# Deformable sampling in single rounds: two PSUM banks cut in quarters, and the steps behind a round set two rounds apart

## The chip, the core and the metric

The kernel runs on one core of one Trainium2 chip. The metric is the device time of one launch in microseconds (us); three runs of the kernel before gave 8797.73, 8817.04 and 8818.68 us, median 8817.04. A core has five engines that each work through their own queue in order: PE (TensorE, matrix products into PSUM), DVE (VectorE), ACT (ScalarE), POOL (GpSimd, here the issuer of gathers) and SP (SyncE, the issuer of plain DMAs). They wait for one another by semaphores, which the Tile framework sets from what each instruction reads and writes.

## What is computed

Four layers on a batch of 4 images of 256 channels and 64 x 64 positions: a block with deformable convolution, linear attention, a 3 x 3 convolution with binarised weights, and a non-local attention block. The change is in the first layer. There each position takes, in each of 4 channel groups, 9 points of a projected image at places that were computed from the data, each by bilinear interpolation, with a softmax weight, and sums them:

```python
x = x + _L0_conv_ref(_gn(x), ...)

# in _L0_conv_ref, of one image in one of G = 4 groups, P = 9 points a position
def tap(xi, yi, w):
    valid = (xi >= 0) & (xi < Wi) & (yi >= 0) & (yi < Hi)
    idx = jnp.clip(yi, 0, Hi - 1) * Wi + jnp.clip(xi, 0, Wi - 1)
    v = jnp.take_along_axis(flat, idx.reshape(B, 1, -1), axis=2)
    v = v.reshape(B, Cc, *xi.shape[1:])
    return v * (w * valid.astype(img.dtype))[:, None]
return tap(x0, y0, (1 - wx) * (1 - wy)) + tap(x0 + 1, y0, wx * (1 - wy)) + tap(x0, y0 + 1, (1 - wx) * wy) + tap(x0 + 1, y0 + 1, wx * wy)

samp = _grid_sample(img, sg)
dout = (samp * mr).sum(-1).reshape(n, G * GC, H * W).transpose(0, 2, 1).reshape(n, H, W, C)
dout = jnp.einsum('nhwc,oc->nhwo', dout, outproj_w) + outproj_b
x2 = _bn(inp + dout, bn2_g, bn2_b, bn2_m, bn2_v, 3)
```

## The kernel before, in words

**Stages.** `run` samples the four images one after another. Beside each sampling, other work is woven in by shares: with image 0 the convolutions and offsets of the other images, with image n the feed-forward and the linear layer of image n - 1, and from image 2 on also the convolution and the attention block of image n - 2. What is left of the last images follows alone. The function `beside` calls the generator `sample` for one round, then lets the other generators go on until they have spent their share, then asks for the next round. Within this part the order of PE, DVE, ACT and POOL is the order in which the program issues instructions (`manual_schedule`); no engine overtakes within its queue.

**A round.** `sample` (L556) takes the 4096 positions of an image in blocks of 224 (`BP`), the last one of 64. A block has 16 rounds of 14 positions (`RP`), the last block 5, with 8 positions in the fifth; so 293 rounds an image and 1172 in all. 14 positions x 9 points are 126 rows. `gathered` (L596) issues four indirect DMAs on POOL (L600), one for each group, which fetch four neighbours of 64 channels for each of the rows into a tile `g` (seven buffers). Then PE multiplies (L607) a sparse weight matrix `wm` (made by DVE at L591 once in four rounds) with `g`: eight products, two accumulating into each of four strips of 32 partitions. The result, 128 x 128 numbers, is a round's sums in `acc`.

**The steps behind a round.** They work on units of two rounds (`UR = 2`). `acc` and `dp` are one PSUM bank each (512 numbers a partition), a single tile cut in two halves that units take in turn (`halves`, L565). For a unit whose last round is number i:

- `moved` (L610): ACT copies the half of `acc` to `at` in SBUF, 128 x 256 (L612). Issued at the start of round i + 1.
- `turned` (L614): PE transposes both rounds of `at` into a half of `dp` (L617). Issued at the start of round i + 2.
- `spread` (L619): ACT copies them to their places in `dT`, the block's transposed sums, in two copies for the two halves of the partitions, 64 x 112 each (L632). Issued at round i + 3, for the first unit of a block one round later. The first one of a block also allots the block's tiles and lets SP load the block of `y`.
- At the end of a block, `project` (L636, PE with the output weights, L640), `add` (DVE, L644) and `finish` (ACT with the batch norm, L649, and the store to `x2_d` on SP, L652), for the two halves of the channels m = 0, 1: project at i + 4 + m, add and finish one and two rounds after it.

`later` (L563) holds, for each round, the list of steps that are due; they are issued at the start of that round ahead of its gathers and matmuls (L658), in the order in which they were put there.

Around the change stand the instructions of the other streams: in the feed-forward PE at L742 and L752, ACT at L744 and DVE at L727; in the linear layer the 25 taps of a depthwise convolution on DVE (L178), transposes and their copies (L862, L863 on PE, L865 on ACT) and products (L869); ACT copies at L823; in layer 2 the products at L1048; in layer 3 the products of the attention (L1147, L1167) and, before them, a PSUM tile whose columns 0 to 127 are written by L1119 and read by ACT at L1122, and whose columns 128 to 255 are written by L1121 and read by DVE at L1123.

Of the kernel before, what the change touches and what calls it, by code (L numbers as in the profile page):

```python
# [9 lines left out]
F32 = mybir.dt.float32  # L10
# [7 lines left out]
P = 128  # L18
N, C, H, W = 4, 256, 64, 64
HW = H * W  # L20
KT = C // P
NB = HW // 512
NT = HW // P
G, PT = 4, 9
# [2 lines left out]
NCH = NT // CT  # L27


RP, WR, UR, BR = 14, 4, 2, 16  # L30
RS, BP = RP * PT, RP * BR
BLOCKS = [(p0, min(BP, HW - p0)) for p0 in range(0, HW, BP)]
OB = 16
# [38 lines left out]
class Net:  # L72
# [483 lines left out]
    def sample(self, n, ssum):  # L556

        nc, sp = self.nc, self.sp
        table = self.tab[n].rearrange("g y x s c -> (g y x) (s c)")
        blocks, images, at, dp, dT, po, later = {}, {}, {}, {}, {}, {}, {}  # L563

        def halves(name):  # L565

            t = self.ps1.tile([P, 2, 256], F32, name=name, tag=name)
            return cycle([t[:, 0], t[:, 1]])

        accs, dps = halves("acc"), halves("dp")  # L570

        def load(b):
            p0, np_ = BLOCKS[b]
            whole, part = np_ // RP, np_ % RP

            nr = whole + (part > 0)
            sl = sp.tile([P, BR, G * 5], F32, name="sl")
            rows = self.s_d[n][p0 * PT:p0 * PT + nr * RS, :].rearrange("(r p) f -> p r f", p=RS)
            more = self.s_d[n][p0 * PT + RS:p0 * PT + (nr + 1) * RS, :].rearrange("(r p) f -> p r f", p=RS)
            nc.sync.dma_start(sl[0:RS, 0:nr], rows)  # L580
            nc.sync.dma_start(sl[RS:P, 0:nr], more[0:P - RS])
            rounds = [(r, RP) for r in range(whole)] + [(whole, part)] * (part > 0)
            blocks[b] = sl, rounds

        def weigh(b, r):

            sl, rounds = blocks[b]
            nu = min(WR, len(rounds) - r)
            wm = self.gp.tile([P, WR, 4 * G, OB], F32, name="wm")
            sh = [P, nu, 4 * G, OB]  # L590
            nc.vector.tensor_tensor(  # L591
                wm[:, 0:nu], self.con("own").unsqueeze(1).unsqueeze(1).to_broadcast(sh),
                sl[:, r:r + nu, G:].unsqueeze(3).to_broadcast(sh), ALU.mult)
            return wm

        def gathered(sl, wm, acc, r):  # L596
            r4, acc = r % WR, acc[:, r % UR * P:(r % UR + 1) * P]
            g = self.gp.tile([P, G, 256], F32, name="g", bufs=7)
            for i in range(G):
                nc.gpsimd.indirect_dma_start(  # L600
                    out=g[:, i, :], out_offset=None, in_=table,
                    in_offset=bass.IndirectOffsetOnAxis(ap=sl.bitcast(I32)[:, r, i:i + 1], axis=0))


            for x in range(2):
                for i in range(G):
                    nc.tensor.matmul(acc[32 * i:32 * i + 32, :], wm[:, r4, 4 * i + 2 * x:4 * i + 2 * x + 2, :],  # L607
                                     g[:, i, x * P:(x + 1) * P], start=x == 0, stop=x == 1)

        def moved(acc, nu, u):  # L610
            at[u] = sp.tile([P, UR, P], F32, name="at")
            nc.scalar.copy(at[u].rearrange("p v c -> p (v c)")[:, 0:nu * P], acc[:, 0:nu * P])  # L612

        def turned(nu, u):  # L614
            dp[u] = next(dps).rearrange("p (v g s o) -> p v g s o", v=UR, g=G, s=2)
            for v in range(nu):
                nc.tensor.transpose(dp[u][:, v].rearrange("p g s o -> p (g s o)"), at[u][:, v], self.ident)  # L617

        def spread(unit, b, u):  # L619

            if b not in dT:
                p0, np_ = BLOCKS[b]
                dT[b] = sp.tile([P, G, BP], F32, name="dT", bufs=1)
                images[b] = sp.tile([P, KT, BP], F32, name="yb")
                nc.sync.dma_start(images[b][:, :, 0:np_], self.y_d[n][:, :, p0:p0 + np_])
            full = sum(1 for _, m in unit if m == RP)
            for v0, v1, m in ((0, full, RP), (full, len(unit), unit[-1][1])):
                for s in range(2):
                    if v0 < v1:
                        hs = slice(64 * s, 64 * s + 64)  # L630
                        q0 = RP * (unit[0][0] + v0)
                        nc.scalar.copy(  # L632
                            dT[b][hs, :, q0:q0 + m * (v1 - v0)].rearrange("p g (v o) -> p g v o", o=m),
                            dp[u][hs, v0:v1, :, s, 0:m].rearrange("p v g o -> p g v o"))

        def project(b, m):  # L636
            np_ = BLOCKS[b][1]
            po[m] = self.ps("po")
            for k in range(G):
                nc.tensor.matmul(po[m][:, 0:np_], self.ow[:, k, m * P:(m + 1) * P], dT[b][:, k, 0:np_], start=k == 0, stop=k == G - 1)  # L640

        def add(b, m):
            ym = images[b][:, m, 0:BLOCKS[b][1]]
            nc.vector.tensor_tensor(ym, po[m][:, 0:BLOCKS[b][1]], ym, ALU.add)  # L644

        def finish(b, m):
            p0, np_ = BLOCKS[b]
            ym = images[b][:, m, 0:np_]
            nc.scalar.activation(ym, ym, AF.Identity, bias=self.sh[:, 4 + m:5 + m],  # L649
                                 scale=self.inv[:, 4 + m:5 + m], accum_out=ssum[:, m, b:b + 1])  # L650
            if m == KT - 1:
                nc.sync.dma_start(self.x2_d[n][:, :, p0:p0 + np_], images[b][:, :, 0:np_])  # L652

        load(0)
        order = [(b, r) for b, (_, np_) in enumerate(BLOCKS) for r in range(-(-np_ // RP))]
        wm = weigh(0, 0)
        for i, (b, r) in enumerate(order):
            for f in later.pop(i, ()):  # L658
                f()
            sl, rounds = blocks[b]  # L660
            if r % UR == 0:
                acc = next(accs)
            gathered(sl, wm, acc, r)
            if r == 0 and b + 1 < len(BLOCKS):
                load(b + 1)
            ends = r + 1 == len(rounds)
            if r % WR == 0:
                if r + WR < len(rounds):
                    nxt = weigh(b, r + WR)
                elif b + 1 < len(BLOCKS):  # L670
                    nxt = weigh(b + 1, 0)
            if r % UR == UR - 1 or ends:
                unit = rounds[r - r % UR:r + 1]
                todo = [partial(moved, acc, len(unit), i), partial(turned, len(unit), i), partial(spread, unit, b, i)]

                todo = [(i + 1 + j + (j == 2 and r < UR), f) for j, f in enumerate(todo)]
                if ends:
                    todo += [(i + 4 + m + j, partial(f, b, m)) for m in range(KT) for j, f in enumerate((project, add, finish))]
                for j, f in todo:
                    later.setdefault(j, []).append(f)  # L680
            if r % WR == WR - 1 or ends:
                wm = nxt
            yield 1
        for i in sorted(later):
            for f in later[i]:
                f()
# [656 lines left out]
```

## The profile before

One profiled execution spans 8805.8 us from its first to its last instruction; the median of the runs is 8817.04 us, so about 11 us lie around the span.

| row of the profile | count | busy us | mean ns | idle before it, us |
|---|---|---|---|---|
| L600 POOL gather | 4688 | 4618.5 | 985 | 2687.8 |
| L607 PE products into acc | 18752 records | 1034.8 | 333 | 1907.8 |
| L612 ACT acc to at, 128 x 256 | 584 | 217.3 | 372 | 985.5 |
| L612 ACT acc to at, 128 x 128 | 4 | 1.1 | 265 | 0.8 |
| L617 PE transposes | 1172 | 284.1 | 330 | 106.6 |
| L632 ACT dp to dT, 64 x 112 | 1168 | 284.4 | 244 | 1041.5 |
| L632 ACT dp to dT, 64 x 32 | 8 | 1.4 | 179 | 2.2 |
| L178 DVE depthwise taps | 2280 | 2933.5 | 1287 | 61.9 |

How to read it: busy is the sum of the bars of a row, and idle the time in which its engine stood still just before them. A row's idle time is ended by another instruction (the releaser), which the profile infers from semaphore events: "PE acc L607 <- ACT at L612: 1273.7, 281, 27.6" means that PE stood still before L607 until the copy at L612 was done, 1273.7 us in all, 281 times, once for 27.6 us. "remote" is a release for which no instruction close in time is seen, "issue" a gap that nothing shown explains. Gaps under 150 ns are not counted. PEld are PE's weight loads, which overlap its products; the two are waited for together, so a list that sums both counts a wait twice. By stretches, with a gather count in brackets in the POOL column (four are a round):

| from to, us | PE busy | DVE busy | ACT busy | POOL busy | granted PE clock |
|---|---|---|---|---|---|
| 250 to 1950 | 826.64 | 757.57 | 244.13 | 1112.59 (1116) | 0.66 |
| 2450 to 3600 | 609.83 | 809.98 | 213.54 | 764.77 (781) | 0.69 |
| 4200 to 5480 | 926.65 | 965.52 | 333.96 | 798.70 (821) | 0.85 |

The gathers stand between 134.1 and 7306.6 us.

### The profile page before, as it was taken

The page shows a single profiled execution, that of the slowest core. Times are in us where ns is not written, and L with a number is a line of the kernel's source. Part 1 is how long each engine was busy: PE and PEld are TensorE (multiplying, and loading weights), DVE is VectorE, ACT ScalarE, POOL GpSimd, SP SyncE. Part 2 cuts the span into 40 slices and gives each one's busy share as a digit, 9 for nine tenths or more (in the row PEclk, how much of TensorE's full clock was granted, in tenths as well). Part 3 has the DMA queues.
Part 4 walks back from the last instruction along what each step waited for, and adds up shares of the span by engine and source line. Part 5 has one row for each costly group of instructions (what it writes and reads, how often), then busy time and mean ns, then how long its engine had stood idle before and what let it go on. Part 6 is the DMA issues. An engine that isn't in the chain of part 4 may idle for free. (4 is left out here: it accounts for less than half of the span.)

```text
span 8805.8 us, 95736 instructions
## 1 busy us (share of the span) xinstructions
PE 5993.9 (68%) x36532; PEld 3575.6 (41%) x36532; DVE 5173.3 (59%) x6409; ACT 2183.8 (25%) x4899; POOL 5152.4 (59%) x4950
## 2 busy tenths in 40 slices
PE   4454554448744446688876677888766778986899
PEld 2222222224323322244544443345544433664477
DVE  5444443443466667424777776227777772599834
ACT  1111111112211112122223222222222222465524
POOL 2666666566666666666666656666666661376410
PEclk7676766669866667799988888898878888998999
DMA  6454454444433334444443344444434343220131
GB/s 172 127 155 124 141 154 118 125 145 145 153 105 105 110 105 129 127 130 138 134 135 110 112 121 136 142 134 132 136 115 117 114 118 99 69 74 29 48 98 53
DMA packets 759050, 1042.27 MB, mean 118 GB/s; under 512 B 362432, under 2 KB 472128, under 8 KB 757056
## 3 DMA queue, kind: packets, MB, share of 16 engines
q0 software_dynamic: 225024, 614.77, 24.3%
q1 hardware_dynamic: 533568, 421.39, 16.4%
q8 instruction: 289, 4.73, 0.2%
q14 instruction: 169, 1.38, 0.0%
HBM read 867.08 MB, written 168.69 MB: 118 GB/s over the span
## 5 line engine op out<-in xcount | busy, mean ns | idle before, releaser
L600 POOL DMA_INDIRECT g<-tab,sl x4688 | 4618.5, 985 | 2687.8 <-issue 1224.2
L178 DVE SCALAR_TENSOR_TENSOR agg<-pad,vec,agg 128x1024 f32<-128x1024 f32 x2280 | 2933.5, 1287 | 61.9
L607 PE MATMUL acc<-g,wm 128*32 128x128 f32 x18752 | 1034.8, 333 | 1907.8 <-ACT at L612 1273.7
L607 PEld LDWEIGHTS acc<-g,wm 128*32 128x32 f32 x18752 | 566.8, 128 | 2411.7 <-ACT at L612 1446.1
L1048 PE MATMUL ps<-xd,w 128*128 128x256 f32 x3072 | 752.7, 396 | 51.3 <-issue 37.8
L591 DVE TENSOR_TENSOR wm<-con,sl 128x1024 f32<-128x1024 f32 (+1 forms) x296 | 357.7, 1209 | 711.9 <-remote 533.5
L1048 PEld LDWEIGHTS ps<-xd,w 128*128 128x128 f32 x3072 | 595.1, 199 | 175.0 <-issue 86.0
L632 ACT COPY dT<-dp 64x112 f32<-64x112 f32 x1176 | 285.9, 243 | 1043.7 <-remote 544.3
L742 PE MATMUL ps<-x2f,f 128*128 128x512 f32 x1024 | 499.2, 636 | 19.1 <-issue 7.7
L817 PE MATMUL ps<-xr,qw 128*128 128x512 f32 x768 | 472.0, 746 | 22.1 <-issue 11.1
L727 DVE SCALAR_TENSOR_TENSOR hm<-ps,vec,lk 128x512 f32<-128x512 f32 x256 | 190.8, 750 | 492.9 <-ACT lk L744 405.5
L752 PE MATMUL ps<-hm,f 128*128 128x512 f32 x1024 | 467.1, 605 | 0.9 <-DVE hm L727 0.9
L612 ACT COPY at<-acc 128x256 f32<-128x256 f32 (+1 forms) x588 | 218.3, 371 | 986.3 <-remote 753.2
L999 POOL TENSOR_TENSOR xd<-xp 128x640 f32<-128x640 f32 x64 | 79.4, 1268 | 492.6 <-ACT xp L1011 298.3
L640 PE MATMUL po<-dT,ow 128*128 128x224 f32 (+1 forms) x1216 | 326.1, 419 | 45.4 <-issue 19.3
L617 PE MATMUL dp<-ident,at 128*128 128x128 f32 x1172 | 284.1, 330 | 106.6 <-ACT dT L632 61.0
L865 ACT COPY kt<-pt 128x512 f32<-128x512 f32 x256 | 149.4, 584 | 829.3 <-remote 403.8
L744 ACT ACTIVATE lk<-ps,low 128x512 f32<-128x512 f32 x256 | 174.0, 687 | 666.0 <-PE ps L742 512.1
L1147 PE MATMUL s<-ph,th 128*128 128x512 f32 x512 | 290.2, 672 | 62.5 <-ACT kt L865 15.9
L640 PEld LDWEIGHTS po<-dT,ow 128*128 128x128 f32 x1216 | 265.5, 233 | 113.8 <-issue 68.9
L1167 PEld LDWEIGHTS ps<-gt,pT 128*128 128x128 f32 x2048 | 276.0, 213 | 70.8 <-issue 46.1
L194 POOL TENSOR_TENSOR ak<-ak,m 128x1024 f32<-128x1024 f32 x96 | 228.1, 2376 | 130.6 <-ACT m L193 126.7
(243 smaller groups left out, 8022.0 us busy)
## 6 DMA issues: line engine op xcount, KB each, us to landing
g<-tab,sl POOLq DMA_INDIRECT x4688
x<-x SPq DMA_DIRECT2D x128, 512.0 KB
xr<-x SPq DMA_DIRECT2D x96, 512.0 KB
tab<-xo SPq DMA_DIRECT2D x192, 128.0 KB
x<-in_x SPq DMA_DIRECT2D x32, 512.0 KB
y<-yc SPq DMA_DIRECT2D x32, 512.0 KB
x2f<-x SPq DMA_DIRECT2D x32, 512.0 KB
xyf<-x SPq DMA_DIRECT2D x32, 512.0 KB
```

The lines of the kernel that those rows point to most:

```text
L178: nc.vector.scalar_tensor_tensor(to, s, wt, acc, ALU.mult, ALU.add)
L591: nc.vector.tensor_tensor(wm[:, 0:nu], self.con("own").unsqueeze(1).unsqueeze(1).to_broadcast(sh), sl[:, r:r + nu, G:].unsqueeze(3).to_bro ...
L600: nc.gpsimd.indirect_dma_start(out=g[:, i, :], out_offset=None, in_=table, in_offset=bass.IndirectOffsetOnAxis(ap=sl.bitcast(I32)[:, r, i: ...
L607: nc.tensor.matmul(acc[32 * i:32 * i + 32, :], wm[:, r4, 4 * i + 2 * x:4 * i + 2 * x + 2, :], g[:, i, x * P:(x + 1) * P], start=x == 0, st ...
L617: nc.tensor.transpose(dp[u][:, v].rearrange("p g s o -> p (g s o)"), at[u][:, v], self.ident)
L632: nc.scalar.copy(dT[b][hs, :, q0:q0 + m * (v1 - v0)].rearrange("p g (v o) -> p g v o", o=m), dp[u][hs, v0:v1, :, s, 0:m].rearrange("p v g ...
L640: nc.tensor.matmul(po[m][:, 0:np_], self.ow[:, k, m * P:(m + 1) * P], dT[b][:, k, 0:np_], start=k == 0, stop=k == G - 1)
L742: nc.tensor.matmul(ps, f1[:, k, m * P:(m + 1) * P], x2[:, k], start=k == 0, stop=k == KT - 1)
L752: nc.tensor.matmul(ps, f2[:, k, m * P:(m + 1) * P], hm[:, k], start=k == 0, stop=k == 4 * KT - 1)
L817: nc.tensor.matmul(ps, qw[:, k, m * P:(m + 1) * P], x[:, k], start=k == 0, stop=k == KT - 1)
L1048: nc.tensor.matmul(ps[:, e], w[:, k, t, 2 * half + e, m * P:(m + 1) * P], v[:, 2 * half + e, k, t:t + 8], start=i % 6 == 0, stop=i % 6 == 5)
L1147: nc.tensor.matmul(s[i], tv[:, 4 * b + j], ph[:, i * 512:(i + 1) * 512], start=True, stop=True)
```

## The change

Units of two rounds are gone: every round has its own copy, transpose and spreading. `acc` and `dp` stay a bank each, a single tile, now cut in four quarters of one round. The copy of round i is issued at the start of round i + 2, its transpose at i + 4, its spreading at i + 6 (rounds 0 and 1 of a block at 8 rounds after them, and at 7), and `project`, `add`, `finish` at i + 7 + m and one and two rounds after, for i the last round of a block. `at` has three buffers of 128 x 128 for two of 128 x 256.

```diff
-RP, WR, UR, BR = 14, 4, 2, 16
+RP, WR, BR = 14, 4, 16
+MOVED, TURNED, SPREAD, PROJECTED = 2, 4, 6, 7
...
-        def halves(name):
+        def quarters(name):
 
-            t = self.ps1.tile([P, 2, 256], F32, name=name, tag=name)
-            return cycle([t[:, 0], t[:, 1]])
+            t = self.ps1.tile([P, 4, P], F32, name=name, tag=name)
+            return cycle([t[:, i] for i in range(4)])
 
-        accs, dps = halves("acc"), halves("dp")
+        accs, dps = quarters("acc"), quarters("dp")
...
-            r4, acc = r % WR, acc[:, r % UR * P:(r % UR + 1) * P]
+            r4 = r % WR
...
-        def moved(acc, nu, u):
-            at[u] = sp.tile([P, UR, P], F32, name="at")
-            nc.scalar.copy(at[u].rearrange("p v c -> p (v c)")[:, 0:nu * P], acc[:, 0:nu * P])
-
-        def turned(nu, u):
-            dp[u] = next(dps).rearrange("p (v g s o) -> p v g s o", v=UR, g=G, s=2)
-            for v in range(nu):
-                nc.tensor.transpose(dp[u][:, v].rearrange("p g s o -> p (g s o)"), at[u][:, v], self.ident)
-
-        def spread(unit, b, u):
+        def moved(acc, u):
+            at[u] = sp.tile([P, P], F32, name="at", bufs=3)
+            nc.scalar.copy(at[u], acc)
+
+        def turned(u):
+            t = next(dps)
+            nc.tensor.transpose(t, at.pop(u), self.ident)
+            dp[u] = t.rearrange("p (g s o) -> p g s o", g=G, s=2)
+
+        def spread(b, r, m, u):
...
-            full = sum(1 for _, m in unit if m == RP)
-            for v0, v1, m in ((0, full, RP), (full, len(unit), unit[-1][1])):
-                for s in range(2):
-                    if v0 < v1:
-                        hs = slice(64 * s, 64 * s + 64)
-                        q0 = RP * (unit[0][0] + v0)
-                        nc.scalar.copy(
-                            dT[b][hs, :, q0:q0 + m * (v1 - v0)].rearrange("p g (v o) -> p g v o", o=m),
-                            dp[u][hs, v0:v1, :, s, 0:m].rearrange("p v g o -> p g v o"))
+            for s in range(2):
+                hs = slice(64 * s, 64 * s + 64)
+                nc.scalar.copy(dT[b][hs, :, RP * r:RP * r + m], dp[u][hs, :, s, 0:m])
...
-            if r % UR == 0:
-                acc = next(accs)
+            acc = next(accs)
             gathered(sl, wm, acc, r)
...
-            if r % UR == UR - 1 or ends:
-                unit = rounds[r - r % UR:r + 1]
-                todo = [partial(moved, acc, len(unit), i), partial(turned, len(unit), i), partial(spread, unit, b, i)]
-
-                todo = [(i + 1 + j + (j == 2 and r < UR), f) for j, f in enumerate(todo)]
-                if ends:
-                    todo += [(i + 4 + m + j, partial(f, b, m)) for m in range(KT) for j, f in enumerate((project, add, finish))]
-                for j, f in todo:
-                    later.setdefault(j, []).append(f)
+            todo = [(MOVED, partial(moved, acc, i)), (TURNED, partial(turned, i)), (SPREAD + max(0, KT - r), partial(spread, b, *rounds[r], i))]
+            if ends:
+                todo += [(PROJECTED + m + j, partial(f, b, m)) for m in range(KT) for j, f in enumerate((project, add, finish))]
+            for j, f in todo:
+                later.setdefault(i + j, []).append(f)
```

## The prediction

> **What bounds the kernel now.** I read the page first (busy times, slices, groups), then the totals of waits, then the timeline of a few rounds, then single lines of code.
>
> The page and the totals of waits:
>
> ```profile
> span 8805.8 us, 95736 instructions
> PE 5993.9 (68%) x36532; PEld 3575.6 (41%) x36532; DVE 5173.3 (59%) x6409; ACT 2183.8 (25%) x4899; POOL 5152.4 (59%) x4950
> L600 POOL DMA_INDIRECT g<-tab,sl x4688 | 4618.5, 985 | 2687.8 <-issue 1224.2
> ...
> PE acc L607 <- ACT at L612: 1273.7, 281, 27.6
> POOL g L600 <- remote: 624.7, 307, 6.0
> POOL g L600 <- PE acc L607: 494.3, 201, 23.2
> ```
>
> No engine is full. Sampling runs from about 134 to 7340 us, 1172 rounds (4688 gathers of four a round), and is 82% of the span. A round's gathers cost POOL at least 4 x (985 + 305 ns) = 5.16 us (305 ns is 1224.2 / 4007, the gap it always has), so 6048 us for all of them; the real pace is (7306.6 - 134.1) / 1172 = 6.12 us. The missing 0.96 us a round is POOL waiting for a free g buffer, which PE frees: the lines "remote" and "PE acc" sum to 1119 us. So PE paces the sampling and POOL follows, seven buffers ahead. And PE's largest wait is the one for the copy at L612. In the timeline:
>
> ```profile
> 2721.80 0.58 ACT L865 COPY kt<-pt 128x512 f32<-128x512 f32 x1 [5.32 <-remote]
> 2721.92 0.94 POOL L600 DMA_INDIRECT g<-tab,sl  x1 [1.83 <-remote]
> 2722.28 0.50 ACT L632 COPY dT<-dp 64x112 f32<-64x112 f32 x2
> 2722.81 0.37 ACT L612 COPY at<-acc 128x256 f32<-128x256 f32 x1
> ...
> 2723.23 1.08 PE L607 MATMUL acc<-g,wm 128*32 128x128 f32 x16 [5.99 <-ACT at L612]
> ...
> 2725.26 0.63 PE L617 MATMUL dp<-ident,at 128*128 128x128 f32 x2
> ...
> 2725.83 1.08 PE L607 MATMUL acc<-g,wm 128*32 128x128 f32 x16
> ```
>
> The matmuls at 2723.23 open a unit. They write the half of the bank that the copy at 2722.81 does not read; their own half was copied a whole unit before. Still they start 50 ns after this copy ends. The second round of the unit (2725.83) waits for nobody. That is the rule and no accident: of the line L607 the trace says
>
> ```profile
>   ACT at L612: 2719.8, 588
> ```
>
> 588 is every unit (PE and weight loads counted together). So the wait is by bank, not by half. The same holds in the other direction, for a read after a write elsewhere in the bank. In layer 3, L1122 reads columns 0 to 127 (written by L1119), L1123 reads 128 to 255 (written by L1121):
>
> ```profile
> L1122 ACT ACTIVATE ph<-ps,fw_add x32: 366/367/378, 4546.1 to 8635.6; 128x128 f32<-128x128 f32 x32
> ...
>   PE ps L1121: 23.8, 17
> ...
>   DVE gt L1123: 43.1, 11
> ```
>
> The read of the first quarter waits for the matmul into the second, and the read of the second waits for the read of the first.
>
> **What the Trainium skill says.** "PSUM — Partial Sum Buffer", PSUM bank collisions: two engines may not touch one bank (in the same partitions) at once, even at different addresses, so waits are to be set by bank; this trace agrees (588 of 588, above). "Perfetto Trace Analysis", Tensor Engine Instruction: the end of a matmul in a profile is computed, and its semaphore comes later, unseen; the trace agrees, for the many waits that end with "remote" end well after the last matmul shown. So a chain PE to ACT to PE costs more than the bars say. "TensorE: Matmul & The Clock Gate", Part 1: a PE idle for some 3.4 us falls to half its clock; here the granted clock is 0.66 from 250 to 1950 us, where PE is busy half the time, and 0.85 from 4200 to 5480. More waiting lengthens what PE does next.
>
> **The change part by part.** Both banks stay one tile each, now in four quarters. In round i the kernel issues, in this order: spread(i-6), two ACT copies out of dp; turned(i-4), a transpose into dp; moved(i-2), an ACT copy out of acc; then the eight matmuls of round i into acc.
>
> *The wait on acc.* By bank, moved(i-2) waits for the matmuls of round i-1, the last writers of its bank, and the matmuls of round i wait for moved(i-2). The distance of two rounds is thus undone; each copy stands between two neighbouring rounds. Before, it stood there once in two rounds: 588 times. Now 1172 times, so 584 are new.
>
> *The wait on dp.* turned(i-4) waits for spread(i-6), spread for turned(i-5). Before, at the odd round, both were long past (L617 waited 61.0 us in all for L632). Now PE meets ACT here too, but at the point where it would wait for moved right after, so this adds order, not a second full wait.
>
> *ACT's work.* Copies: 1172 x 265 ns (the four 128x128 ones there are) = 310.6, for 218.3 now: +92 us. Spreads: 2344 of 64x56 for 1176 of 64x112. The rows have 179 ns for 64x32 and 244 for 64x112, so about 198 ns: 465 for 286, +179 us. ACT at 25% has room, but these stand in its queue just ahead of what PE waits for.
>
> *PE's and POOL's work.* 1172 transposes, 18752 matmul records and 4688 gathers, as before: nothing. Gathers and the wm products (L591) are not moved.
>
> *The sum.* When ACT comes on time, a meeting costs PE the stretch from the first spread to the first matmul: 2722.28 to 2723.23 = 0.95 us a unit now. After: 2 x 0.198 + 0.265 + 0.08 of gaps = 0.74 a round, 1.48 for two rounds. That is +0.53 us x 588 = +312 us. Behind each image the deeper pipeline drains without rounds between, six stages for two, about a meeting each: 4 x 0.74 x 4 images = +12 us. POOL's waits show that lateness of PE reaches the gathers, so I count it whole: +325 us.
>
> Bounds: below, 0, if ring and ACT's idle time swallow it. Above, each new meeting costs what a present one does, when ACT is late with its other queue (kt, lk, v copies stand ahead of it): 1273.7 / 588 = 2.17 us, x 584 = +1265 us. I don't take that, because much of it is ACT's backlog of two rounds, which would be met half at a time. What waits behind the stopped PE: the transposes and products of the feed-forward, linear and convolution streams, and through L742 to L744 and L727 DVE. Behind the stopped ACT: the same streams' copies.
>
> *Moves.* Projection, add and finish come three rounds later; the loads of y (SP) and the stores of x2 with them, both a block (16 rounds) from use. The new spread waits for the last project of the block before, as now one round back. Both at nothing; if SP were late, add would show it.
>
> The profiled span is 8805.8, the median of the runs 8817.0, 11 us more. 8805.8 + 325 + 11 = 9142, say 9150 us.
>
> **The rivals.**
>
> A, forecast, one meeting a round at about its bare price: 9150 (own range 8950 to 9500). Chance 0.50.
>
> B, full price. ACT is late as often as now, at every round: 8817 + 1265 = 10080. For: half of PE's openings wait, with 4.5 us each (1273.7 / 281). Against: ACT's backlog is halved. With values between A and B, 0.16.
>
> C, swallowed. POOL's 5.16 us a round stays the floor and PE's new stops fall where it stood idle anyway: in 250 to 1950 PE is busy 49% and yet the pace is 6.09 us, in 4200 to 5480 72% at 6.24, so the pace hardly follows PE's load. 8817 to 8930. Chance 0.21, of which 0.06 within 0.3%, 0.02 slightly faster.
>
> D, faster: the waits are by quarter after all. Then moved(i-2) finds its matmuls done a round ago, and ACT never stops for the newest ones (753.2 + 141.0 us before L612 now), nor PE for the newest copy (1273.7). Gain at most POOL's 1119 us of waiting; a third, since PE's other waits remain: 8817 - 370 = 8450. It decides if fewer than half of the rounds wait for their newest neighbour. Against: 588 of 588 and L1122. Chance 0.13.
>
> **How the numbers follow.** Faster 0.13 + 0.02 = 0.15; same 0.06; slower 0.50 + 0.16 + 0.13 = 0.79. About 0.3% (26 us) is what a measurement here can tell from no change. The range leaves out D (0.13) and the upper part of B (0.07): 8800 to 9700 us.
>
> **What would show it.** Right: L607 waits for the copy some 1172 times, with more than 1273.7 us; the new copies take about 265 and 198 ns; POOL's "remote" and "PE acc" grow by about what the span grows. A wrong: the count stays near 588, or it doubles and POOL's waits don't grow (C), or the mean wait stays 2.2 us (B). Wrong altogether: PE's waits for ACT shrink (D), or the copies are far from the prices.

## The result and the profile after

The changed kernel takes 8942.99 us (median of 4 runs, 8916.39 to 8947.37), the kernel before 8817.86 (8797.73 to 8839.72) measured beside it. The medians differ by 125 us. The ratio is put at 1.0126 with a 95% interval of 1.0102 to 1.0151, that is 90 to 133 us. The forecast had the sign, and the wait for the newest copy, but counted 325 us.

The page of the changed kernel; a row has count, busy us and mean ns, and after the bar the idle time of the engine ahead of it with what ended most of it:

```profile
span 8940.6 us, 98293 instructions
PE 6060.7 (68%) x36532; PEld 3589.3 (40%) x36532; DVE 5177.0 (58%) x6409; ACT 2415.7 (27%) x6651; POOL 5164.5 (58%) x4950
...
L601 POOL DMA_INDIRECT g<-tab,sl x4688 | 4631.3, 988 | 2808.2 <-issue 1210.8
...
L608 PE MATMUL acc<-g,wm 128*32 128x128 f32 x18752 | 986.8, 340 | 1041.5 <-ACT at L613 709.3
L617 PE MATMUL dp<-ident,at 128*128 128x128 f32 x1172 | 421.1, 359 | 1238.5 <-ACT dT L629 902.5
...
L613 ACT COPY at<-acc 128x128 f32<-128x128 f32 x1172 | 311.6, 266 | 1717.6 <-remote 1262.5
...
L629 ACT COPY dT<-dp 64x56 f32<-64x56 f32 x2344 | 466.2, 199 | 630.2 <-remote 261.5
```

ACT works 231.9 us more and still only 27% of the span. The two copies cost 266 and 199 ns, where 265 and 198 were estimated. PE's stop has moved: most of it now stands ahead of the transpose (1238.5 us, 106.6 before) and less ahead of the products (1041.5, 1907.8 before). Together 2280.0 us, 265.6 more than the 2014.4 of before.

From the totals of waits of the changed kernel (us in all, times, longest):

```profile
PE dp L617 <- ACT dT L629: 902.5, 340, 17.2
PE acc L608 <- ACT at L613: 709.3, 187, 28.6
POOL g L601 <- PE acc L608: 623.2, 237, 30.4
POOL g L601 <- remote: 587.4, 300, 5.8
```

POOL's two waits for a free buffer sum to 1210.6 us, 91.6 more than before. One round in the timeline shows the meeting (start, duration, engine, line; in brackets the idle time and what ended it):

```profile
4704.32 0.40 ACT L629 COPY dT<-dp 64x56 f32<-64x56 f32 x2
...
4704.74 0.27 ACT L613 COPY at<-acc 128x128 f32<-128x128 f32 x1
...
4704.77 0.47 PE L617 MATMUL dp<-ident,at 128*128 128x128 f32 x1 [1.54 <-ACT dT L629]
...
4705.18 1.08 PE L608 MATMUL acc<-g,wm 128*32 128x128 f32 x16
...
4706.56 0.95 POOL L601 DMA_INDIRECT g<-tab,sl  x1 [7.79 <-PE acc L608]
```

PE stands until both spreads are done, transposes while ACT copies, and starts the products after the copy: 0.86 us from the first spread to the first product, 0.74 in the estimate. The whole trace shows the same order: in all 1164 rounds that have such a copy ahead of them (the first two of each image have none) the products start after it has ended, in 610 of them within 0.1 us. Before, all 587 openings of a unit did so, 428 within 0.1 us. So the mechanism is there, in every round.

Where the time went is seen by stretches. POOL's counts in brackets, almost all gathers (four a round), tell how far each kernel came in the same stretch; the stretches are the first three images of the kernel before. Kernel before, then changed kernel:

```profile
134.00:1949.00 1815.00, 853.55 (x6730) 491.38 (x6734) 797.73 (x1062) 250.10 (x695) 1189.60 (x1195) 0.65 0.48 136
1949.00:3703.00 1754.00, 1048.70 (x6865) 549.29 (x6865) 1048.42 (x1046) 343.85 (x877) 1159.32 (x1173) 0.74 0.42 123
3703.00:5522.00 1819.00, 1366.94 (x8670) 819.14 (x8669) 1147.13 (x1373) 453.97 (x1108) 1144.58 (x1173) 0.87 0.44 128
```

```profile
134.00:1949.00 1815.00, 840.83 (x6692) 491.24 (x6692) 794.41 (x1051) 300.85 (x1120) 1181.37 (x1187) 0.64 0.48 136
1949.00:3703.00 1754.00, 1061.27 (x6763) 548.91 (x6764) 1049.23 (x1046) 397.01 (x1296) 1141.39 (x1156) 0.73 0.41 121
3703.00:5522.00 1819.00, 1351.97 (x8489) 806.92 (x8488) 1138.63 (x1362) 504.63 (x1514) 1120.28 (x1141) 0.86 0.43 126
```

(columns: us, then busy time and count of PE, weight loads, DVE, ACT and POOL, then PE's granted clock, DMA share and GB/s.) In the stretch of image 0 the changed kernel falls 8 gathers behind, in image 1 17, in image 2 32. The loss grows with what runs beside the sampling. Read from the start of the last round of each image, the four samplings became longer by 16, 20, 47 and 47 us, 131 in all. The rest of the span, after the last round, went from 1476.0 to 1479.9 us.

### The profile page after: what moved, and what is told of

Its sections match the earlier page's. It is cut to its first block, busy times and chain, and to the rows that moved or that the text cites. A ratio compares the mean times of both kernels' runs of the same rounds, so it can differ in the third digit from the quotient of the medians.

```text
span 8940.6 us, 98293 instructions
## 1 busy us (share of the span) xinstructions
PE 6060.7 (68%) x36532; PEld 3589.3 (40%) x36532; DVE 5177.0 (58%) x6409; ACT 2415.7 (27%) x6651; POOL 5164.5 (58%) x4950
## 5 line engine op out<-in xcount | busy, mean ns | idle before, releaser
L608 PE MATMUL acc<-g,wm 128*32 128x128 f32 x18752 | 986.8, 340 | 1041.5 <-ACT at L613 709.3
L617 PE MATMUL dp<-ident,at 128*128 128x128 f32 x1172 | 421.1, 359 | 1238.5 <-ACT dT L629 902.5
L608 PEld LDWEIGHTS acc<-g,wm 128*32 128x32 f32 x18752 | 554.8, 130 | 1377.8 <-ACT at L613 841.1
L617 PEld LDWEIGHTS dp<-ident,at 128*128 128x128 f32 x1172 | 188.0, 160 | 1678.9 <-ACT dT L629 1151.9
L613 ACT COPY at<-acc 128x128 f32<-128x128 f32 x1172 | 311.6, 266 | 1717.6 <-remote 1262.5
L629 ACT COPY dT<-dp 64x56 f32<-64x56 f32 x2344 | 466.2, 199 | 630.2 <-remote 261.5
```

The costliest lines, as they stand in the source:

```text
L617: nc.tensor.transpose(t, at.pop(u), self.ident)
L629: nc.scalar.copy(dT[b][hs, :, RP * r:RP * r + m], dp[u][hs, :, s, 0:m])
```

## The experiments

All ratios are against the kernel before, run in the same group of runs on the same chip; intervals in brackets are 95%. This matters here: on the chips of e1 to e8 and e13 to e16 the kernel before took 8764 to 8826 us, on that of e9 to e12, e17 and e18 7739 us. So runs of different groups are compared by ratio, or not at all.

### What a meeting costs: its length, its number, its distance

**e1.** ACT's finer instructions in the kernel before.

```diff
-            nc.scalar.copy(at[u].rearrange("p v c -> p (v c)")[:, 0:nu * P], acc[:, 0:nu * P])
+            for v in range(nu):
+                nc.scalar.copy(at[u][:, v], acc[:, v * P:(v + 1) * P])
...
-            for v0, v1, m in ((0, full, RP), (full, len(unit), unit[-1][1])):
+            for v0, v1, m in [(v, v + 1, unit[v][1]) for v in range(len(unit))]:
```

> The kernel before, with ACT's instructions cut as fine as in the changed kernel (the copy of a unit in two of 128x128, the spreads in four of 64x56), in the same places, so still 588 meetings of PE and ACT at acc. The stretch that PE is held at a meeting when ACT comes on time grows from 0.95 to about 4 x 0.198 + 2 x 0.265 + 0.1 = 1.42 us. Theory 1, length: a meeting costs its stretch in full, as the forecast counted: +0.47 us x 588 = +276, 9093 us. Theory 2, share: only some two fifths of a stretch arrive at the end (125 of 312 us in the change): about +110, 8930. Theory 3, number: what costs is the doubled number of meetings and not ACT's work in them: 8820 to 8835.

Measured: 1.0072 (1.0058 to 1.0086), about +64 us. Of the 276 us by which the stretches were estimated to grow, a quarter arrived. All three theories were off: length counts, but at far below its price.

**e2** and **e3.** The order of the steps in a round turned over, in the changed kernel and in the kernel before: `moved`, `turned`, `spread`. Projection, add and finish, where they fall into the same round, now go ahead of these three.

```diff
-            for f in later.pop(i, ()):
+            for f in sorted(later.pop(i, ()), key=lambda f: ("moved", "turned", "spread").index(f.func.__name__) if f.func.__name__ in ("moved", "turned", "spread") else -1):
                 f()
```

> The changed kernel, with the three steps of a round issued in the opposite order: copy out of acc, then transpose, then the two spreads. PE no longer waits for the spreads of its own round, only for the copy; the stretch of a meeting shrinks from 0.74 to about 0.35 us, their number stays 1172. Theory 1, length: -0.39 us x 1172 = -457, about 8490 us. Theory 2, share of two fifths: -180, about 8760. Theory 3, number: no change, 8943.

> The kernel before with the copy out of acc issued ahead of the two spreads that fall into the same round. The stretch of a meeting shrinks from 0.95 to about 0.45 us, their number stays 588. Theory 1, length: -0.5 us x 588 = -294, 8523 us. Theory 2, share: -118, about 8700. Theory 3, number: no change, 8817.

Measured: e2 1.0055 (1.0041 to 1.0068), so about 47 to 63 us of the change's loss come back (the changed kernel had 1.0126 and, in e13, 1.0108), where 457 were to come by length in full. e3 0.9974 (0.9963 to 0.9984), 23 us faster where 294 were to come. A stop made shorter gives about a tenth of what it is shortened by.

**e4.** The distances back to one round.

```diff
-MOVED, TURNED, SPREAD, PROJECTED = 2, 4, 6, 7
+MOVED, TURNED, SPREAD, PROJECTED = 1, 2, 3, 4
```

> The changed kernel with its steps one round apart (1, 2, 3, project at 4) in place of two. Theory A, order by bank: the distance counts for nothing, since each copy stands between two neighbouring rounds anyway; same within 0.3% of 8943 us, perhaps 10 less for the shorter drain. Theory B, the two rounds' distance gives part of the extra cost back (transposes and spreads find their input long ready): some 100 us slower than the changed kernel, 9040.

Measured: 1.0159 (1.0141 to 1.0178), an interval that overlaps with the changed kernel's 1.0102 to 1.0151, but not with that of its second measurement, on another chip (e13, 1.0091 to 1.0125). So the two rounds' distance bought between nothing and about half a per cent, some 45 us, and not the 100 us of theory B. Theory A is the nearer one; that the distance counts for nothing is not shown.

### What sets the pace

**e5** and **e6.** One of the four gathers of each round left out, in the kernel before and in the changed kernel.

```diff
-            for i in range(G):
+            for i in range(G - 1):
                 nc.gpsimd.indirect_dma_start(
...
-                                     g[:, i, x * P:(x + 1) * P], start=x == 0, stop=x == 1)
+                                     g[:, min(i, G - 2), x * P:(x + 1) * P], start=x == 0, stop=x == 1)
```

> The kernel before without the fourth gather of each round (group 3's products read group 2's rows: a quarter of the fetched data is left out). POOL's floor falls from 5.16 to 3 x 1.29 = 3.87 us a round. Theory P, PE's waits pace the sampling (step 1 of the prediction): 8700 to 8817 us. Theory G, gathers and their landing pace it together with PE: well below, 8000 to 8500 us.

> The changed kernel with the same gather left out. If POOL's floor is what swallowed the meetings, the change costs far more once the floor is out of the way: 250 to 330 us over the kernel before with three gathers. If PE's own idle time (late completions) swallowed them, the difference stays about 125 us.

Measured: e5 0.8658 (0.8628 to 0.8687), 7642.33 us: 1172 us less, 1.0 us a round for a gather that holds POOL 1.29. e6 0.8834 (0.8804 to 0.8864), 153 us over e5. So gathers are on the path, and with POOL's floor lowered to 3.87 us the change costs hardly more than before. POOL's floor alone did not swallow the meetings. Nor does POOL's own time set the pace there: in e5 a round took (6135.2 - 134.9) / 1172 = 5.12 us, well above that floor, and POOL still stood for free buffers, 1472.8 us in all against 1119.0 before:

```profile
POOL g L600 <- PE acc L607: 1194.7, 475, 33.7
...
POOL g L600 <- remote: 278.1, 155, 3.1
```

With a gather less, PE gave the buffers back sooner. The last section shows what may lie behind this.

**e7** and **e8.** Half of the products left out.

```diff
-            for x in range(2):
+            for x in range(1):
                 for i in range(G):
...
-                                     g[:, i, x * P:(x + 1) * P], start=x == 0, stop=x == 1)
+                                     g[:, i, x * P:(x + 1) * P], start=True, stop=True)
```

> The kernel before with four of the eight products of a round (the two left neighbours of each point are kept, the two right ones left out). The bars of L607 cover 0.88 us a round. Theory bars: they shrink by half, 0.44 us x 1172 = 516 us at most, of which a quarter to two fifths arrive as in the experiments before: 8600 to 8700 us. Theory hidden: the products take several us a round beyond their bars, and PE waits that out at the meetings; then half of it goes, and the time falls towards POOL's floor of 5.16 us a round: 7700 to 8200 us.

> The changed kernel with the same four products left out. If the meetings were swallowed by the products' hidden end, the change costs another amount here: with POOL at its floor in most rounds it is worth less, 0 to 60 us over the kernel before with half the products; if it is worth its bare price wherever it stands, 300 us; if the same two fifths, 125.

Measured: e7 0.9995 (0.9983 to 1.0008), e8 1.0116 (1.0081 to 1.0152), 113 us over e7. Half of the products are worth nothing. The row of the products in e7:

```profile
L607 PE MATMUL acc<-g,wm 128*32 128x128 f32 x9376 | 627.7, 341 | 2138.3 <-ACT at L612 1577.1
```

The bars are 407 us shorter than before, and the wait for the same copies is 303 us longer (1273.7 before). The time that the products no longer need has mostly become waiting. This run takes the first step of the prediction away, that PE paces the sampling, as far as it means the products that the bars show. One thing is not separated: PE's granted clock was 0.78 here against 0.81, which may have slowed PE's other work.

**e10**, **e14**, **e15.** The kernel before with each bank holding the sums of a unit and the transposes of another, the units taking the banks in turn, so that PE writes one while ACT reads the other. The steps also stand two rounds apart, as in the change; the kernel before was not run with this distance alone. e14 is e10 again, on another chip; e15 adds the finer ACT work of e1.

```diff
-        accs, dps = halves("acc"), halves("dp")
+        one, two = ([next(h), next(h)] for h in (halves("acc"), halves("dp")))
+        accs, dps = cycle([one[0], two[0]]), cycle([one[1], two[1]])
...
-                todo = [(i + 1 + j + (j == 2 and r < UR), f) for j, f in enumerate(todo)]
+                todo = [(i + 1 + 2 * j + (j == 2 and r < UR), f) for j, f in enumerate(todo)]
...
-                    todo += [(i + 4 + m + j, partial(f, b, m)) for m in range(KT) for j, f in enumerate((project, add, finish))]
+                    todo += [(i + 7 + m + j, partial(f, b, m)) for m in range(KT) for j, f in enumerate((project, add, finish))]
```

> The kernel before with its two banks used otherwise: each bank holds the sums of a unit in its first half and a transposed unit in its second, the units take the banks in turn, and the transposes and spreads are issued 3 and 5 rounds after a unit (project at 7), so that PE writes one bank while ACT reads the other. The wait for the newest copy (1273.7 us in the profile before) loses its reason: PE has a whole unit of time for it. Theory P, PE's waits for ACT are on the path: several hundred us faster, 8300 to 8500. Theory S, they lie in time that PE would stand anyway, and a tenth to a quarter of 588 x 0.95 us is all there is to gain: 8680 to 8800.

> The kernel before with its banks swapped by unit, as in e10, on the chip of this call. Theory P (waits for ACT are on the path where PE is late for the gathers): on a chip of about 8820 us several hundred us faster than the kernel before. Theory S: 0.5 to 1.5% faster on any chip.

> e14 with ACT's instructions cut as fine as in the changed kernel (copies of 128x128, spreads of 64x56: 229 us more of ACT's time), with no meeting of PE and ACT on a bank in use. If the finer work costs by standing inside the meetings: no more than 15 us over e14. If it costs as ACT's load on the other streams: the 64 us it cost in e1, or more.

Measured: e10 0.9906 (0.9890 to 0.9923), e14 0.9894 (0.9878 to 0.9911), e15 0.9904 (0.9886 to 0.9921). Both chips agree on 1%. In e14, the largest waits of PE at the products, and POOL's for buffers (the sums lie in both tiles now, so L608 appears as acc and as dp):

```profile
PE acc L608 <- issue: 433.9, 593, 2.6
PE dp L608 <- issue: 416.9, 542, 3.1
```

```profile
POOL g L601 <- remote: 579.2, 271, 5.6
...
POOL g L601 <- PE dp L608: 196.9, 92, 19.7
POOL g L601 <- PE acc L608: 189.9, 67, 22.6
```

ACT is no longer among the larger waits of the products. A wait of 1273.7 us has gone, and the kernel is 86 us faster. The products still stand 850.8 us for nothing that the profile shows (492.9 before), and POOL waits 966.0 us for buffers (1119.0 before). And e15 takes 8679.26 us to e14's 8678.05: ACT's finer work, 64 us inside the meetings of e1, costs nothing measurable outside one. Against e15, which has the changed kernel's ACT work and no such meeting, the changed kernel (e13) loses 189 us.

**e9.** Five buffers for seven (`bufs=7` to `bufs=5` for `g`).

> The kernel before with five buffers for the gathers in place of seven. POOL's gather of a round starts about 37 us before PE's products on it (six rounds). Theory ring: that lead is what a round needs to come through, so five buffers stretch the pace by up to 7/5: up to 2800 us slower. Theory late release: the lead is only a full ring, PE gives buffers back at its own pace whatever their number: 8817 us within 1%.

Measured: 1.0066 (1.0049 to 1.0083), 53 us. This run doesn't decide what it was made for: it fell on the chip of 7739 us, and there PE started a round a median 1.7 us after its data had landed, so the ring of buffers was not full. In its totals of waits PE stands for the gathers, which it hardly ever did in the trace of before (29.5 us, 8 times):

```profile
PE acc L607 <- DMA g<-tab,sl: 664.1, 792, 21.1
```

### Without the gathers, and with nobody waiting for them

**e11**, **e12**, **e16.** A plain load by SP in place of a round's gathers; e16 is e11 again, on another chip.

```diff
-            for i in range(G):
-                nc.gpsimd.indirect_dma_start(
-                    out=g[:, i, :], out_offset=None, in_=table,
-                    in_offset=bass.IndirectOffsetOnAxis(ap=sl.bitcast(I32)[:, r, i:i + 1], axis=0))
+            nc.sync.dma_start(g, table.rearrange("(a t) c -> a (t c)", t=2)[4 * P * r:4 * P * (r + 1), :].rearrange("(i p) f -> p i f", p=P))
```

> The kernel before with each round's four gathers on POOL replaced by one plain load of as many bytes issued by SP, from rows in their order (the sampled addresses are left out). Theory P, PE's own work and waits pace a round: 8600 to 8817 us. Theory G, POOL's gathers pace it: far below, 6500 to 7500 us, where PE's other work is the bound.

> The changed kernel with the same replacement. If the gathers are what hides the meetings, the bare price of the forecast shows here: +0.53 us x 588 = 312 us over the kernel before with plain loads, or more. If the meetings cost what they cost in the change wherever they stand: +125 us.

> The kernel before with plain loads by SP in place of the four gathers (the sampled addresses are left out), on the chip of this call. On a chip where the kernel before takes about 8820 us: if it is POOL's gathers that make the two chips differ, the time is that of the other chip, 7050 to 7100 us; if the chips differ otherwise, it keeps the difference, 7900 to 8200 us.

Measured: e11 7063.63 us, 0.9130 (0.9114 to 0.9145); e12 7231.04, 0.9341 (0.9326 to 0.9357); e16 7063.07, 0.8054 (0.8039 to 0.8069). The two chips, 1025 us apart with the gathers, agree within 1 us without them. e12 is 167 us over e11, neither the 312 nor the 125 of the two theories. In e12's page the wait for the spreads stands ahead of the transpose, as in the changed kernel (928.6 us, 902.5 there), and the products hardly wait any more:

```profile
L617 PE MATMUL dp<-ident,at 128*128 128x128 f32 x1172 | 394.4, 337 | 953.0 <-ACT dT L629 928.6
L608 PE MATMUL acc<-g,wm 128*32 128x128 f32 x18752 | 874.8, 312 | 205.4 <-DMA g<-tab 89.7
```

**e17** and **e18.** All gathers are made, but the products read a fixed tile.

```diff
+        fixed = self.gp.tile([P, G, 256], F32, name="fixed", bufs=1)
+        nc.vector.memset(fixed, 0.5)
...
-            g = self.gp.tile([P, G, 256], F32, name="g", bufs=7)
+            g = self.gp.tile([P, G, 256], F32, name="g", bufs=6)
...
-                                     g[:, i, x * P:(x + 1) * P], start=x == 0, stop=x == 1)
+                                     fixed[:, i, x * P:(x + 1) * P], start=x == 0, stop=x == 1)
```

> The kernel before with all its gathers, but with the products reading one fixed tile in place of what was fetched (the sampled values are left out; six buffers for gathers and the fixed tile for seven). POOL no longer waits for PE and PE no longer for the gathers. Theory R, the buffers' release sets the pace: POOL runs at its floor (1172 x 5.16 = 6048 us), and the time falls to that of the plain loads or a little more, 7050 to 7300 us. Theory C, issuing gathers slows the other engines: still above 8000 us on a chip where the kernel before takes about 8800.

> The changed kernel with the same cut. If the tie to POOL hid the meetings, they cost their bare price here, about 312 us over the kernel before with loose gathers. If the lateness is shared among the meetings whatever paces, about what it was with plain loads, 130 to 190 us.

Measured, on the chip of 7739 us: e17 0.9980 (0.9970 to 0.9989), e18 1.0165 (1.0148 to 1.0182), 142 us over e17. POOL's largest wait in e17 is its own gap, and its wait for buffers is gone:

```profile
POOL g L602 <- issue: 1425.9, 4681, 0.3
```

On this chip POOL runs at its floor, tied to PE or not: its gathers end at 6168 us, (6168.3 - 134) / 1172 = 5.15 us a round, against 5.16 in the prediction. Neither theory's number came: R had nothing to gain on this chip, and C's condition (one of about 8800) wasn't met. Whether the buffers' release or the gathers themselves make the other chips slower was not tried.

**e13** is the changed kernel unaltered.

> The changed kernel unaltered, on the chip of this call. On a chip where the kernel before takes about 8820 us: 1.4% over it, as before. On one where it takes about 7740 us, PE is seldom late for the gathers: theory S (POOL hides the meetings) expects less than there, 20 to 80 us over the kernel before; theory L expects about as much as with plain loads, 130 to 170 us.

Measured: 8868.32 us over 8763.78, 1.0108 (1.0091 to 1.0125). It fell on one of the slower chips; the changed kernel with its own gathers was not run on the faster one.

### The price by image

The length of the sampling of each image, changed kernel minus kernel before, from the starts of the last rounds in the traces (us). The bare price of the meetings over one image is 312 / 4 = 78. Each row is one execution of each kernel, and whole executions of one kernel lie 10 to 42 us apart, so a difference of 10 or 20 us in a cell is not safe:

| pair | image 0 | 1 | 2 | 3 | sum |
|---|---|---|---|---|---|
| the two kernels | 16 | 20 | 47 | 47 | 131 |
| three gathers (e6, e5) | 15 | 14 | 58 | 56 | 143 |
| half the products (e8, e7) | -8 | 35 | 33 | 41 | 101 |
| plain loads (e12, e11) | 10 | 32 | 75 | 73 | 190 |
| loose gathers (e18, e17) | -1 | 10 | 59 | 70 | 138 |

Without gathers, images 2 and 3 pay 75 and 73 us of the 78 (68 and 73 if e16 is taken for e11; the traced execution of e12 was 15 us above its median). There the sampling of a round takes 1534 / 293 = 5.2 us, PE is busy 82% of it in e16, and the stops arrive almost in full. In image 1 PE is busy 69% and 32 us arrive; in image 0 it is 62% (648.90 of 1040 us), 10 us arrive, and something else set the end. With gathers that nobody waits for, images 0 and 1 pay 9 together: POOL's floor, 5.15 us a round or some 1510 an image, is longer than the 1041 and 1326 us that these images took with plain loads.

## Why the prediction went wrong

**The sum, "I count it whole", is the term that failed.** The prediction counted +0.53 us x 588 = 312 us alike over all four images; 131 arrived in the traces, 42%. The first half of the step held: PE's idle time before the two rows grew by 266 us, near the 312. The second half did not: only half of these 266 us reached the end. By image, 60% of the bare price arrived in images 2 and 3 (47 of 78), about a quarter or less in 0 and 1 (16 and 20). That the rest fell into time in which PE was not what the end waited for follows from the pairs above; no trace shows it stop by stop. The prediction gave the argument itself, under rival C (pace hardly follows PE's load; PE 49% busy in the first stage and 72% in a later one), and then chose one answer for the whole. Taken by stage, with A for images 2 and 3 and C for 0 and 1, its own numbers would have given about 2 x 78 and little more, some 160 to 180 us. That is said in hindsight, and it is still above 131: why images 2 and 3 pay 47 beside gathers and 73 to 75 with plain loads stays open.

**PE paces the sampling (first part).** Wrong, if it means PE's work and its waits as the page lists them. e7 takes half of the products away for no gain, e14 takes PE's wait for ACT away for 1%, and a gather less is worth 1.0 us a round (e5). POOL waiting for a buffer that PE frees showed who came last, not that PE's time was short. And most of PE's largest wait was not ACT's doing. Of the 1273.7 us that PE stood for the copy at L612, ACT itself stood 771 us until an update of PE's semaphore that came more than 1 us after the end shown of PE's work (of the 476.8 us of the same wait in e9, none). So PE waited, by way of ACT, for the late signal of its own completion. Taking ACT out of the way, as e14 does, leaves that lateness in place.

**The wait by bank.** Right, and shown three ways: the copies stand between neighbouring rounds (all 1164 of them), the distance makes little difference (e4, about half a per cent), and swapped banks remove the wait (e14). The Trainium skill, "PSUM — Partial Sum Buffer", PSUM bank collisions, asks for waits to be set by bank and not by address, and the traces agree. In these kernels each bank is also one tile of the program; whether the waits follow the bank or the tile, no run separates.

**The count.** The prediction read the 588 in `ACT at L612: 2719.8, 588` as every unit. It is a sum of two lists, PE's 281 waits and the 307 of its weight loads, and meets the number of units by chance:

```profile
PEld acc L607 <- ACT at L612: 1446.1, 307, 28.1
PE acc L607 <- ACT at L612: 1273.7, 281, 27.6
```

So about half of the openings showed a wait. The order by bank holds all the same, as the starts of all 587 show, but the forecast of some 1172 waits of L607 stands on the misreading. PE itself waited for the copy 187 times in the changed kernel, and 340 times for the spreads ahead of the transpose: 527 against 281 + 27 = 308 before. PE now meets ACT first at the transpose. So "adds order, not a second full wait" held for the sum (+266 us in both), but the place was misjudged: the wait on dp became the larger one.

**ACT's prices.** Right (266 and 199 ns; 778 us of copies and spreads, 504 before). e15 shows that this work costs only inside a meeting; within one, e1 puts it at 64 us, about half of the change's loss. The other half is then what the doubled number brings, by difference, if the two simply add.

**Drain and moves.** 12 us for the drains: after the last image it is 4, the other three are inside the table's figures. Moves at nothing: the add (L639) waited 112.6 us for remote releases and 47.8 for PE's projection, 160.4, against 153.2 before. That holds.

**The rivals.** C had the size (8817 to 8930, measured 8943, just above) and part of the reason. D needed waits by quarter; in none of the 1164 rounds do the products start before the newest copy has ended. B needed each new meeting at 2.17 us: the mean stop per round fell from 2014.4 / 588 = 3.4 us a unit to 2280.0 / 1172 = 1.9 us a round, so lateness was shared, as argued against B.

**Better than both.** The swapped banks (e10, e14) are 0.9906 and 0.9894 of the kernel before. They keep units of two rounds and give PE and ACT a bank each, with the steps further apart.

## What to carry to other kernels

Price a new stop stage by stage: it arrives almost in full where the stopping engine sets the pace of that stage (75 of 78 us with plain loads), and in small part elsewhere, even where its waits are the largest on the page. A test for this is cheap: halve the engine's own work and see whether the time moves. Follow a large wait one step further, too: ask what the engine that is waited for was itself waiting for. And a tile cut into quarters of one PSUM bank is one buffer for two engines; what separates them is which bank each uses at a time, not how many rounds lie between.

## What the runs showed of the hardware

The same program took 8764 to 8826 us on three chips and 7739 us on a fourth; with plain loads in place of POOL's gathers one of the three and the fourth agree within 1 us (7063.07 and 7063.63). A gather held POOL as long on both (985 ns in the profile of before, 980 in e9). By the DMA packets in the traces, PE starts a round a median 27 us (e14) to 30 us (before) after its last gather's data landed on the slower chips, the ring being full, and 1.7 us on the faster one (e9).

What differs stands in the traces, which also keep the times at which semaphores were updated. How late an update of PE's semaphore is, is counted here from the last shown end of a PE instruction that updates it. In the profile of before, 1111 of 3713 recorded updates come more than 1 us late, 268 of them more than 5 us; for ACT's and for DVE's own semaphore it is 2 each. In all traces from slower chips with gathers, 601 (e6) to 1865 (e7) are over 1 us late. In every trace of the faster chip, and in e16, a slower chip with plain loads, it is 2. Fewer products do not make it less (e7); one gather less in four does (e5, 617).

One such place, in the kernel before around 1001 us:

```profile
1001.00 1.23 DVE L591 TENSOR_TENSOR wm<-con,sl 128x1024 f32<-128x1024 f32 x1 [13.16 <-remote]
1001.05 0.37 ACT L612 COPY at<-acc 128x256 f32<-128x256 f32 x1 [10.23 <-remote]
1001.24 1.81 POOL L600 DMA_INDIRECT g<-tab,sl  x1 [2.06 <-remote]
...
1001.48 1.08 PE L607 MATMUL acc<-g,wm 128*32 128x128 f32 x16 [10.60 <-issue]
```

The last instruction that PE shows ahead of this ended at 990.88. Three engines that by the program wait for its products (for buffers of wm and g, for sums in acc) start within 0.3 us of each other. All three wait for PE's semaphore, and the trace has an update of it at 1000.98, 10.1 us after that end. The page says "remote" because no shown instruction ends close to it. The Trainium skill, "Perfetto Trace Analysis", Tensor Engine Instruction, says that a matmul's end is computed and its semaphore comes later, unseen; the traces agree, and here show how much later.

POOL's last gather ahead of this began at 998.23 and took 0.95 us. That is common: 206 of the 268 updates over 5 us late come when POOL has stood for more than 0.4 us since its last gather, a state that fills 15% of the sampling. Whether the gathers hold PE's completion back, or POOL only stands because it waits for PE, whether PE finished late or only its signal came late, and why one chip shows none of it, no run here shows. It fits e7, where half of the products changed nothing, and e5; that it is the cause of either is argued, not shown.
